# One-hot products of a source's three parts added in one PSUM bank, in a graph network kernel on one core

## The chip, the cores and the metric

The kernel runs on one core of a Trainium2 chip. The metric is the device time of one execution in microseconds (us); the times before and after are medians over runs. The engines are PE (the matrix engine, with its weight loads listed as PEld), DVE (vector), ACT (scalar), POOL and SP; SP and POOL also issue the transfers (DMAs). PE accumulates into PSUM, eight banks of 2 KB per partition, from which ACT and DVE copy results out.

## The reference

A graph of 6250 nodes (128 features) and 206250 edges, sorted by destination. Three attention layers (GATv2), then a small network, each with a residual and a layer norm:

```python
xl = (x @ Wl + bl).reshape(n, heads, outc)
e_feat = leaky_relu(xl[src] + (x @ Wr + br).reshape(n, heads, outc)[dst], 0.2)
logits = einsum('ehc,hc->eh', e_feat, att)
a = exp(logits - segment_max(logits, dst)[dst])
a = a / segment_sum(a, dst)[dst]
out = segment_sum(xl[src] * a[:, :, None], dst) + bias     # 4, 4 and 1 heads
...
e_aggr = segment_sum(edge_attr, dst) / maximum(count, 1)   # 96 edge features
h = concat([x, e_aggr, u[batch]]) @ W1 + b1                # 256 columns
h = relu(batch_norm(h)) @ W2 + b2
```

Everything is float32. The costly part is `xl[src]`: each destination needs the transformed rows of its 33 sources on average.

## The kernel before

**Blocks and slots.** The nodes are ranked by how many sources need a gather and cut into 49 blocks of 128 destinations, one per partition (`NB = 49`). A destination's sources lie in slots. Sources are divided by node number into 16 windows of 3 blocks of 128 nodes (the last of 4). Of each window a destination's first source goes into a window slot; all other sources go into its rest list, whose length `KR[b]` is 9 to 47 by block. So a block has 17 slots in the tile `ga` (its own row and 16 window slots) and `KR[b]` gathered slots in the tiles `g`.

**Window slots without a gather** (`windows`, L662). The table `tab` in SBUF holds all 49 source blocks, each value as a sum of three bf16 parts (`table`, L894: a cast on ACT L904, a subtraction on DVE L906, and so on, three parts in turn for up to `TS = 6` blocks at a time). A one-hot matrix `oh` of a block and window selects the row. PE multiplies one-hot by table block, 128 x (3 x 132) columns into a bank `pg` (L681), adding the window's three blocks there (129 in place of 132 columns in the last layer, with one head). ACT casts the bank to bf16 `raw` (L683); the three parts of three windows are then added by three products with a bf16 identity into the bank `ps` (L670), which ACT copies to `ga` (L671). The eight PSUM banks are: `pa` 2, `pt` 1, `pp` 2, `pg` 2, `ps` 1.

**Gathered slots** (`gather`, L631): one indirect transfer per slot, issued by POOL (L639), from the rows of all nodes in DRAM.

**The steps.** Each layer runs over the 49 blocks, in program order on each engine (an order written out by hand, nothing is moved). A step works on several blocks at once: `n2` (two ahead) starts its gathers and its windows 0 to 8, `c` gets its weights (exp on ACT, L714) and its weighing (`weigh`, L716: multiplications on DVE L722, sums over slots on PE L726), `c0` (one behind) is combined (moments with a square root on ACT L139, used by DVE at L144) and multiplied for the next layer (transpose L162, ACT L167, products L168 and L169, copy L171); then `n2`'s windows 9 to 15. The logits of `n1` (one ahead) stand on DVE in three pieces between these (L696 to L700). The order within a step:

```python
if c: c.weights()
if n2: n2.windows(tab, n2.oh, range(0, WH))
if n1: n1.logits(slice(1, 2))
if c: c.weigh()
if c0: c0.combine()
...
if c0: c0.output(); c0.products()
if n2: n2.windows(tab, n2.oh, range(WH, NW))
```

In the first layer each step also fetches a block's record (L776), unpacks it (L780) and builds its one-hots on DVE; later layers load the one-hots from DRAM. Every third step edge features are loaded (L846) and summed (L873). In the last layer the residual and the small network's hidden products (L1037 to L1054) hang on each step.

**The prologue** (up to 551 us) finds the sources of each node from the sorted edges and classifies them in seven groups of seven blocks (`classify`, L374): window slots by a masked maximum, the rest list by pairs of MAX (eight largest, L401) and MATCH_REPLACE (L403) up to `KL = 48` entries. It also computes layer 1's products (`first_sources`, L340), checks that the destinations are sorted (L432) and ranks the nodes. After it come the opening of the first layer (small memsets L812 to L817, records, loads, table) and then the steps; each later layer has its own opening with loads and a new table.

Of the kernel before, what the change touches and what calls it, by code (L numbers as in the profile page):

```python
# [20 lines left out]
P = 128  # L21
N, E, F, FE = 6250, 206250, 128, 96
NB = (N + P - 1) // P
NPAD = NB * P
# [9 lines left out]
WB = 3  # L34
NW = NB // WB
# [9 lines left out]
ROFF = tuple(sum(KR[:b]) for b in range(NB + 1))  # L45
KMAX = max(KD)
KEY = 128
KL = 48
RCLIP = KR[0] + 1
NBIN = RCLIP + 2  # L50
NT = (E + P - 1) // P
# [9 lines left out]
def chunks(b):  # L61

    n = min(EP, KM[b]) or EP
    r = KD[b] - n
    m = -(-r // EP)
    return [(0, n)] + [(n + r * i // m, r * (i + 1) // m - r * i // m) for i in range(m)]


TL = 13
TS = 6  # L70
WH = 9
TPW = P + max(LW)

# [14 lines left out]
def gnn_kernel(ctx: ExitStack, tc: tile.TileContext, t, out):  # L88
# [11 lines left out]

    ident = const.tile([P, P], F32, name="ident")
    make_identity(nc, ident)
    identb = const.tile([P, P], BF16, name="identb")
    nc.vector.tensor_copy(identb, ident)
# [14 lines left out]
    rec = dram.tile([NPAD, RW], F32, name="rec")  # L119

    ox = [None] + [dram.tile([NPAD, LW[l]], F32, name=f"ox{l}") for l in (1, 2)]
    ohd = dram.tile([NPAD, NB * P], BF16, name="ohd")
    pkd = dram.tile([NB * NW, P], BF16, name="pkd")
    hd = dram.tile([P, 2, NPAD], F32, name="hd")
# [53 lines left out]
    degs = const.tile([P, NB], F32, name="degs")  # L178
    first = const.tile([P, NB], F32, name="first")
    nfast = const.tile([P, 1], I32, name="nfast")  # L180
    bparts, wcat, attb, cbc, gcol, vs3 = ([] for _ in range(6))
    with tc.tile_pool(name="pre", bufs=1) as rp, tc.tile_pool(name="prew", bufs=2) as rw, \
            tc.tile_pool(name="n0", bufs=3) as np0, tc.tile_pool(name="n0p", bufs=2, space=PSUM) as npp, \
# [181 lines left out]
                nc.gpsimd.memset(wc[:, 1, w:w + 1], float(N - WBLK[w][0] * P - 256 + 1000))  # L365

        def rank_constants():
            for b in range(NB):
                nc.gpsimd.memset(kr[:, b:b + 1], float(KR[b]))
                nc.gpsimd.memset(kd[:, b:b + 1], float(KD[b]))  # L370
                nc.gpsimd.memset(km[:, b:b + 1], float(min(EP, KM[b])))
            nc.gpsimd.memset(onesq, 1.0)

        def classify(q):  # L374
# [19 lines left out]
            for j in range(UQ):  # L394
                v = key[:, j, :]
                s = 0
                for w in range(0, NW, 8):
                    nc.vector.match_replace(rest[:, j, s, :], top[:, j, w:w + 8], v, 0.0)
                    v, s = rest[:, j, s, :], 1 - s
                for k in range(0, KL, 8):  # L400
                    nc.vector.max(lst[:, j, k:k + 8], v)  # L401
                    if k + 8 < KL:
                        nc.vector.match_replace(rest[:, j, s, :], lst[:, j, k:k + 8], v, 0.0)  # L403
                        v, s = rest[:, j, s, :], 1 - s
            cls = rw.tile([P, UQ, CW_], F32, name="cls")
            any_ = rw.tile([P, UQ, NW], F32, name="any_")
            nc.vector.tensor_tensor(any_, top, wc[:, 0:1, :].to_broadcast([P, UQ, NW]), op=ALU.is_ge)
# [21 lines left out]
        bad = rp.tile([P, 5], F32, name="bad")  # L429
        falls = rp.tile([PP, W], BF16, name="falls")  # L430

        def sorted_check():  # L432
# [3 lines left out]
            nc.vector.memset(bad, 0.0)  # L436
            nc.vector.tensor_tensor(falls, d2[:, 1:], d2[:, :W], op=ALU.is_lt)
            nc.vector.tensor_reduce(bad[:PP, 0:1], falls, AX.X, ALU.max)

# [10 lines left out]
        for q in range(NQB):  # L450
            if q + 1 < NQB:
                find(q + 1, wins[q + 1])
            degrees(q)
            if q + 2 < NQB:
                wins.append(search(q + 2))
            if q == 0:
                finish += [weights(1), weights(2)]
            if q + 1 < NQB:
                for b in range((q + 1) * UQ, (q + 2) * UQ):
                    first_sources(b)  # L460
            classify(q)
            if q == 0:
                finish[1]()
                finish[2]()
            if q == 1:
                sorted_check()
                rank_constants()
# [140 lines left out]
    class Block:  # L608
# [52 lines left out]

        def windows(self, tab, oh, ws):  # L662


            k, X = self.k, self.X

            def add(w0, n, raw):
                ps = k.ps.tile([P, 3, X], F32, name="ps", padded_shape=[P, 3, XM])
                for i in range(3):
                    nc.tensor.matmul(ps[:, :n, :], lhsT=identb, rhs=raw[:, :n, i, :], start=i == 0, stop=i == 2)  # L670
                nc.scalar.copy(self.ga[:, 1 + w0:1 + w0 + n, :], ps[:, :n, :])  # L671

            todo = None
            for w0 in range(ws.start, ws.stop, 3):
                n = min(3, ws.stop - w0)
                raw = k.raw.tile([P, 3, 3, X], BF16, name="raw", padded_shape=[P, 3, 3, XM])
                for w in range(w0, w0 + n):
                    pg = k.pg.tile([P, 3, X], F32, name="pg", padded_shape=[P, 3, XM])
                    for j, s in enumerate(WBLK[w]):
                        o = j * NW + w if j < WB else WB * NW + j - WB  # L680
                        nc.tensor.matmul(pg, lhsT=oh[:, o, :], rhs=tab[:, s, :, :],  # L681
                                         start=j == 0, stop=s == WBLK[w][-1])
                    nc.scalar.copy(raw[:, w - w0, :, :], pg)  # L683
                    if todo:
                        add(*todo)
                        todo = None
                todo = w0, n, raw
            add(*todo)

        def logits(self, which):  # L690

# [68 lines left out]
    def slots_path():  # L760

        with ExitStack() as s:
            k = Pools(s, "sl", (("one", 1, 0), ("ga", 3, 0), ("big", 6, 0), ("wk", 2, 0), ("wk3", 3, 0),
                                ("ohp", 2, 0), ("pa", 2, 1), ("pt", 1, 1), ("pp", 2, 1), ("pg", 2, 1),
                                ("ps", 1, 1), ("raw", 2, 0)))
            one = k.one


# [4 lines left out]
            def record(c):  # L773

                c.rc = k.rcp.tile([P, RW], F32, name="rc")
                nc.gpsimd.indirect_dma_start(  # L776
                    out=c.rc, out_offset=None, in_=rec,
                    in_offset=bass.IndirectOffsetOnAxis(ap=ids_i[:, c.b:c.b + 1], axis=0))

            def unpack(c):  # L780
                b, o = c.b, LW[0] + F
                nc.sync.dma_start(out=rows(xp, b), in_=c.rc[:, LW[0]:o])
                nc.scalar.copy(sres[:, ROFF[b]:ROFF[b + 1]], c.rc[:, o:o + KR[b]])
# [23 lines left out]
                nc.sync.dma_start(out=c.oh.rearrange("p j d -> p (j d)"), in_=rows(ohd, c.b))  # L807


            NE = max(len(chunks(b)) for b in range(NB))  # L810
            off, cap = (one.tile([P, NE, NB], F32, name=v) for v in ("off", "cap"))
            nc.gpsimd.memset(off, 0.0)  # L812
            nc.gpsimd.memset(cap, float(E - EP))
            for b in range(NB):
                for i, (o, n) in enumerate(chunks(b)):
                    nc.gpsimd.memset(off[:, i, b:b + 1], float(o))
                    nc.gpsimd.memset(cap[:, i, b:b + 1], float(E - n))  # L817
# [75 lines left out]

            def table(l, c, loads):  # L894

                tab = one.tile([P, NB, 3, F + HEADS[l]], BF16, name="tab", padded_shape=[P, NB, 3, XM])
                done = 0
                for q, m, tf in loads:
                    for p in range(0, m, TS):
                        u = min(TS, m - p)  # L900
                        x = tf[:, p:p + u, :]
                        for i in range(3):
                            part = tab[:, q + p:q + p + u, i, :]
                            nc.scalar.copy(part, x)  # L904
                            if i < 2:
                                nc.vector.tensor_sub(x, x, part)  # L906
                        n = NW if q + p + u == NB else (q + p + u) // WB
                        n -= (n - done) % 3 if n < NW else 0
                        if n > done:
                            c.windows(tab, c.oh, range(done, n))  # L910
                            done = n
                return tab

            def layer(l, between, end):
# [589 lines left out]
```

## Time and profile before

| | |
|---|---|
| median of 17 runs | 7128.93 us (7098.39 to 7156.67) |
| the profiled execution | 7120.84 us |
| its span | 7119.0 us |
| mean granted clock of PE | 0.809 |
| busiest engine | DVE, 4560.9 us |
| products of the windows (L681) | 7203, 1698.0 us busy |
| casts of them (L683) | 2352, 1131.6 us busy |
| identity products (L670) and copies (L671) | 2646, 625.3 us, and 882, 398.3 us busy |
| gathers' issues (L639) | 2796, 2676.0 us busy |

The span runs from the first to the last instruction. Busy time is a sum over instructions; matmuls overlap, and their ends are modelled. In a list of waits, "sd L144 <- ACT sd L139" means that the engine stood idle before L144 until L139 on ACT was done; "issue" is idle time that no wait in the profile explains, and "remote" a release whose sender could not be found. In a timeline the bracket gives idle time ahead of an instruction and what ended it. The granted clock is given in parts of full speed.

### The profile page before, as it was taken

The numbers are of one execution on the slowest core, as the hardware profiler recorded it, in microseconds if no ns is written. First come the engines' busy times: TensorE is split into PE (matmuls) and PEld (weight loads), VectorE is DVE, ScalarE is ACT, GpSimd is POOL, SyncE is SP. The second block draws the span as 40 slices with busy tenths as digits, with TensorE's granted clock in tenths as the row PEclk, the third lists the DMA queues.
The fourth block names the chain that finished last, engine by engine and source line by source line (L and its number), as shares of the span: only waits on it lengthen the run. The fifth ranks groups of instructions, "written<-read, shape, count | busy, mean of one in ns | idle before, by whom it ended". The sixth has DMA issues, their size and how long they took to land. (4 is left out here: it accounts for less than half of the span.)

```text
span 7119.0 us, 52212 instructions
## 1 busy us (share of the span) xinstructions
PE 4119.3 (58%) x15200; PEld 2024.4 (28%) x15200; DVE 4560.9 (64%) x6804; ACT 2389.8 (34%) x5024; POOL 3132.3 (44%) x3642
## 2 busy tenths in 40 slices
PE   2214646545666655565655566665657665666665
PEld 1112223222223322222322233332323332333333
DVE  7875657656667756565755666665667676676665
ACT  3203324323333333333433234333333332333332
POOL 4314453454444443445454444544444444444442
PEclk9996878777788877787877788887788887888877
DMA  2203333334333323333334333333333334333332
GB/s 61 60 18 112 102 90 109 102 94 94 99 106 106 118 86 111 81 91 89 96 87 87 98 87 101 89 103 84 92 92 100 99 87 90 101 100 86 97 89 85
DMA packets 307927, 654.28 MB, mean 92 GB/s; under 512 B 93492, under 2 KB 215367, under 8 KB 283954
## 3 DMA queue, kind: packets, MB, share of 16 engines
q0 software_dynamic: 116720, 302.44, 18.0%
q1 hardware_dynamic: 186482, 341.98, 14.2%
q10 hardware_dynamic: 4432, 6.43, 0.3%
q8 instruction: 126, 2.06, 0.1%
q14 instruction: 167, 1.37, 0.1%
HBM read 519.06 MB, written 131.50 MB: 91 GB/s over the span
## 5 line engine op out<-in xcount | busy, mean ns | idle before, releaser
L639 POOL DMA_INDIRECT g<-xl,sres x2796 | 2676.0, 957 | 2350.7 <-issue 879.9
L681 PE MATMUL pg<-tab,oh 128*128 128x396 bf16 (+1 forms) x7203 | 1698.0, 376 | 1234.0 <-ACT raw L683 555.8
L683 ACT CAST raw<-pg 128x396 bf16<-128x396 f32 (+1 forms) x2352 | 1131.6, 489 | 1645.4 <-remote 883.4
L681 PEld LDWEIGHTS <-oh 128*128 128x128 bf16 x7203 | 770.9, 108 | 2016.9 <-issue 1653.8
L670 PE MATMUL ps<-raw,identb 128*128 128x396 bf16 (+1 forms) x2646 | 625.3, 351 | 692.5 <-issue 336.3
L722 DVE TENSOR_TENSOR ga<-ga,q 128x2176 f32<-128x2176 f32 x147 | 355.3, 2417 | 850.1 <-ACT q L714 495.6
L699 DVE TENSOR_REDUCE q<-z 128x68 f32<-128x2176 f32 (+19 forms) x444 | 777.6, 1751 | 15.3
L697 DVE SCALAR_TENSOR_TENSOR z<-z,q 128x2176 f32<-128x2176 f32 (+11 forms) x444 | 774.2, 1744 | 15.3
L671 ACT COPY ga<-ps 128x396 f32<-128x396 f32 (+1 forms) x882 | 398.3, 452 | 730.6 <-remote 285.5
L726 PE MATMUL acc<-ga,ident 128*128 128x512 f32 (+1 forms) x1470 | 615.0, 568 | 42.9 <-issue 29.0
L726 PE MATMUL acc<-g,ident 128*128 128x512 f32 (+3 forms) x1590 | 625.1, 541 | 0.0
L670 PEld LDWEIGHTS <-identb 128*128 128x128 bf16 x2646 | 274.1, 106 | 1021.3 <-issue 913.2
L846 POOL DMA_INDIRECT g<-in_ea_dram,est_i x102 | 96.7, 948 | 973.3 <-PE acc L726 696.5
L696 DVE TENSOR_TENSOR z<-g,q 128x1152 f32<-128x1152 f32 (+12 forms) x297 | 418.6, 1410 | 81.1 <-DMA g<-xl,sres 34.3
L144 DVE RECIPROCAL sd<-sd 128x1 f32<-128x1 f32 x196 | 31.0, 158 | 654.9 <-ACT sd L139 593.8
L726 PEld LDWEIGHTS acc<-ga,ident 128*128 128x128 f32 x1470 | 298.2, 205 | 373.8 <-issue 359.6
L722 DVE TENSOR_TENSOR g<-g,q 128x1280 f32<-128x1280 f32 (+8 forms) x243 | 400.7, 1682 | 0.0
L873 PE MATMUL acc<-g,ident 128*128 128x480 f32 (+4 forms) x818 | 378.0, 623 | 15.5 <-issue 13.5
L168 PE MATMUL tp<-wcat,hT 128*128 128x260 f32 (+1 forms) x294 | 141.0, 572 | 395.3 <-ACT hT L167 323.3
L726 PEld LDWEIGHTS acc<-g,ident 128*128 128x128 f32 x1590 | 286.6, 190 | 281.0 <-issue 273.5
L696 DVE TENSOR_TENSOR z<-ga,q 128x2176 f32<-128x2176 f32 x147 | 353.7, 2406 | 0.2
L167 ACT ACTIVATE hT<-tp,gcol 128x128 f32<-128x128 f32 x98 | 44.8, 457 | 820.4 <-PE tp L162 433.7
(259 smaller groups left out, 3587.6 us busy)
## 6 DMA issues: line engine op xcount, KB each, us to landing
oh<-ohd SPq DMA_DIRECT2D x98, 1568.0 KB
ohd<-oh SPq DMA_DIRECT2D x49, 1568.0 KB
g<-xl,sres POOLq DMA_INDIRECT x2796
pr<-pkd SPq DMA_DIRECT2D x49, 512.0 KB
rec<-lin SPq DMA_DIRECT2D x49, 130.0 KB
ox<-lin SPq DMA_DIRECT2D x49, 130.0 KB
ox<-lin SPq DMA_DIRECT2D x49, 128.5 KB
xrs<-ox SPq DMA_DIRECT2D x98, 64.0 KB
```

What stands on the lines that cost most here:

```text
L168: nc.tensor.matmul(pl, lhsT=hT, rhs=wcat[l], start=True, stop=False)
L639: nc.gpsimd.indirect_dma_start(out=g[:, i, :], out_offset=None, in_=xl[self.l], in_offset=bass.IndirectOffsetOnAxis(ap=sres[:, j:j + 1], a ...
L670: nc.tensor.matmul(ps[:, :n, :], lhsT=identb, rhs=raw[:, :n, i, :], start=i == 0, stop=i == 2)
L671: nc.scalar.copy(self.ga[:, 1 + w0:1 + w0 + n, :], ps[:, :n, :])
L681: nc.tensor.matmul(pg, lhsT=oh[:, o, :], rhs=tab[:, s, :, :], start=j == 0, stop=s == WBLK[w][-1])
L683: nc.scalar.copy(raw[:, w - w0, :, :], pg)
L696: nc.vector.tensor_add(z, g[:, :, :F], self.xrb.unsqueeze(1).to_broadcast([P, n, F]))
L697: nc.vector.scalar_tensor_tensor(z, z, 0.0, self.att.unsqueeze(1).to_broadcast([P, n, F]), op0=ALU.max, op1=ALU.mult)
L699: nc.vector.tensor_reduce(lg[:, cs, :], z.rearrange("p k (h c) -> p k h c", h=H), AX.X, ALU.add)
L722: nc.vector.tensor_mul(gh, gh, lg[:, c:c + n, :].unsqueeze(3).to_broadcast([P, n, H, F // H]))
L726: nc.tensor.matmul(self.acc[:, :r, :], lhsT=ident, rhs=g[:, i:i + r, :F], start=c + i == 0, stop=c + i + r == K1)
L873: nc.tensor.matmul(self.acc[:, :r, :], lhsT=ident, rhs=ea[:, i:i + r, :], start=o + i == 0, stop=o + i + r == K)
```

## The change

- **Windows.** The three parts are no longer three column ranges of one product. For each window PE makes one product of 128 x 132 for each source block and part, and all nine (twelve in the last window) add into the same slot of a bank. Three windows lie in one bank `pg`, and ACT copies the bank to `ga`. The bf16 identity, the tile `raw`, the bank `ps`, the casts and the identity products are gone; `pg` has three banks. A block has 147 products in place of 49 + 18.
- **Rest lists.** `KL` is 24 in place of 48: three pairs of MAX and MATCH_REPLACE per block. What is left over is stored to DRAM (`rst`). The six blocks with more than 24 rest sources fetch that row with a further gather (`record`) and extract the remaining entries when they are unpacked.
- **Prologue and opening.** The small memsets of the edge offsets move from the first layer's opening to `rank_constants`; the load for the check of the order moves ahead of the check; the first products of block 48 move behind the classification of the sixth group.
- **Table.** `TS` is 7, so there are 8 groups in place of 11, and the three parts of neighbouring groups are interleaved: each turn does part 1 of a group, part 2 of the one before and part 3 of the one before that. The first block's windows follow one turn later.

```diff
-KL = 48
+KL = 24
-TS = 6
+TS = 7
...
         def rank_constants():
+            nc.gpsimd.memset(eoff, 0.0)
+            nc.gpsimd.memset(ecap, float(E - EP))
             for b in range(NB):
...
+                for i, (o, n) in enumerate(chunks(b)):
+                    nc.gpsimd.memset(eoff[:, i, b:b + 1], float(o))
+                    nc.gpsimd.memset(ecap[:, i, b:b + 1], float(E - n))
...
                 for k in range(0, KL, 8):
                     nc.vector.max(lst[:, j, k:k + 8], v)
-                    if k + 8 < KL:
-                        nc.vector.match_replace(rest[:, j, s, :], lst[:, j, k:k + 8], v, 0.0)
-                        v, s = rest[:, j, s, :], 1 - s
+                    nc.vector.match_replace(rest[:, j, s, :], lst[:, j, k:k + 8], v, 0.0)
+                    v, s = rest[:, j, s, :], 1 - s
+            nc.sync.dma_start(out=rst[q * UQ * P:(q + 1) * UQ * P, :].rearrange("(b p) f -> p b f", p=P),
+                              in_=rest[:, :, 1 - s, :])
...
             if q == 0:
                 finish += [weights(1), weights(2)]
+                sorted_load()
             if q + 1 < NQB:
-                for b in range((q + 1) * UQ, (q + 2) * UQ):
+                for b in range((q + 1) * UQ, min((q + 2) * UQ, NB - 1)):
                     first_sources(b)
             classify(q)
+            if q + 2 == NQB:
+                first_sources(NB - 1)
...
         def windows(self, tab, oh, ws):
             k, X = self.k, self.X
-            def add(w0, n, raw):
-                ps = k.ps.tile([P, 3, X], F32, name="ps", padded_shape=[P, 3, XM])
-                for i in range(3):
-                    nc.tensor.matmul(ps[:, :n, :], lhsT=identb, rhs=raw[:, :n, i, :], start=i == 0, stop=i == 2)
-                nc.scalar.copy(self.ga[:, 1 + w0:1 + w0 + n, :], ps[:, :n, :])
-            todo = None
             for w0 in range(ws.start, ws.stop, 3):
                 n = min(3, ws.stop - w0)
-                raw = k.raw.tile([P, 3, 3, X], BF16, name="raw", padded_shape=[P, 3, 3, XM])
+                pg = k.pg.tile([P, 3, X], F32, name="pg", padded_shape=[P, 3, XM])
                 for w in range(w0, w0 + n):
-                    pg = k.pg.tile([P, 3, X], F32, name="pg", padded_shape=[P, 3, XM])
-                    for j, s in enumerate(WBLK[w]):
+                    todo = [(j, i) for j in range(len(WBLK[w])) for i in range(3)]
+                    for j, i in todo:
                         o = j * NW + w if j < WB else WB * NW + j - WB
-                        nc.tensor.matmul(pg, lhsT=oh[:, o, :], rhs=tab[:, s, :, :],
-                                         start=j == 0, stop=s == WBLK[w][-1])
-                    nc.scalar.copy(raw[:, w - w0, :, :], pg)
-                    if todo:
-                        add(*todo)
-                        todo = None
-                todo = w0, n, raw
-            add(*todo)
+                        nc.tensor.matmul(pg[:, w - w0, :], lhsT=oh[:, o, :], rhs=tab[:, WBLK[w][j], i, :],
+                                         start=(j, i) == todo[0], stop=(j, i) == todo[-1])
+                nc.scalar.copy(self.ga[:, 1 + w0:1 + w0 + n, :], pg[:, :n, :])
...
+                if KR[c.b] > KL:
+                    c.keys = k.rcp.tile([P, 2, KMAX], F32, name="keys", bufs=1)
+                    nc.gpsimd.indirect_dma_start(
+                        out=c.keys[:, 0, :], out_offset=None, in_=rst,
+                        in_offset=bass.IndirectOffsetOnAxis(ap=ids_i[:, c.b:c.b + 1], axis=0))
...
             def table(l, c, loads):
                 tab = one.tile([P, NB, 3, F + HEADS[l]], BF16, name="tab", padded_shape=[P, NB, 3, XM])
-                done = 0
-                for q, m, tf in loads:
-                    for p in range(0, m, TS):
-                        u = min(TS, m - p)
-                        x = tf[:, p:p + u, :]
-                        for i in range(3):
-                            part = tab[:, q + p:q + p + u, i, :]
-                            nc.scalar.copy(part, x)
-                            if i < 2:
-                                nc.vector.tensor_sub(x, x, part)
+                groups = [(q + p, tf[:, p:min(p + TS, m), :]) for q, m, tf in loads for p in range(0, m, TS)]
+                done = ready = 0
+                for i in range(len(groups) + 3):
+                    upto = ready
+                    for part in range(3):
+                        if 0 <= i - part < len(groups):
+                            o, x = groups[i - part]
+                            to = tab[:, o:o + x.shape[1], part, :]
+                            nc.scalar.copy(to, x)
+                            if part < 2:
+                                nc.vector.tensor_sub(x, x, to)
+                            else:
+                                ready = o + x.shape[1]
...
```

More of the change, by code (lines that the diff above doesn't have):

```diff
@@ L102, in gnn_kernel @@
     make_identity(nc, ident)
-    identb = const.tile([P, P], BF16, name="identb")
-    nc.vector.tensor_copy(identb, ident)
     ones = const.tile([1, P], F32, name="ones")
@@ L121, in gnn_kernel @@
     ox = [None] + [dram.tile([NPAD, LW[l]], F32, name=f"ox{l}") for l in (1, 2)]
+    rst = dram.tile([NPAD, KMAX], F32, name="rst")
     ohd = dram.tile([NPAD, NB * P], BF16, name="ohd")
@@ L180, in gnn_kernel @@
     nfast = const.tile([P, 1], I32, name="nfast")
+    NE = max(len(chunks(b)) for b in range(NB))
+    eoff, ecap = (const.tile([P, NE, NB], F32, name=v) for v in ("eoff", "ecap"))
     bparts, wcat, attb, cbc, gcol, vs3 = ([] for _ in range(6))
@@ L430, in gnn_kernel, with sorted_load @@
         falls = rp.tile([PP, W], BF16, name="falls")
-        def sorted_check():
+        def sorted_load():
             nc.sync.dma_start(out=d2[:, :W], in_=t["dst"].rearrange("(p w) -> p w", p=PP))
@@ L436, in sorted_check @@
             nc.vector.memset(bad, 0.0)
+        def sorted_check():
             nc.vector.tensor_tensor(falls, d2[:, 1:], d2[:, :W], op=ALU.is_lt)
@@ L763, in slots_path @@
             k = Pools(s, "sl", (("one", 1, 0), ("ga", 3, 0), ("big", 6, 0), ("wk", 2, 0), ("wk3", 3, 0),
-                                ("ohp", 2, 0), ("pa", 2, 1), ("pt", 1, 1), ("pp", 2, 1), ("pg", 2, 1),
-                                ("ps", 1, 1), ("raw", 2, 0)))
+                                ("ohp", 2, 0), ("pa", 2, 1), ("pt", 1, 1), ("pp", 2, 1), ("pg", 3, 1)))
             one = k.one
@@ L782, in unpack @@
                 nc.sync.dma_start(out=rows(xp, b), in_=c.rc[:, LW[0]:o])
-                nc.scalar.copy(sres[:, ROFF[b]:ROFF[b + 1]], c.rc[:, o:o + KR[b]])
+                n = min(KL, KR[b])
+                nc.scalar.copy(sres[:, ROFF[b]:ROFF[b] + n], c.rc[:, o:o + n])
+                if KR[b] > KL:
+                    m = KR[b] - KL
+                    mr = -(-m // 8) * 8
+                    lst = k.rcp.tile([P, 32], F32, name="lst", bufs=1)
+                    for i in range(0, mr, 8):
+                        a = i // 8 % 2
+                        nc.vector.max(lst[:, i:i + 8], c.keys[:, a, :])
+                        if i + 8 < mr:
+                            nc.vector.match_replace(c.keys[:, 1 - a, :], lst[:, i:i + 8], c.keys[:, a, :], 0.0)
+                    lst_i = k.rcp.tile([P, 32], I32, name="lst_i", bufs=1)
+                    nc.vector.tensor_copy(lst_i[:, :m], lst[:, :m])
+                    nc.vector.tensor_scalar(lst_i[:, :m], lst_i[:, :m], KEY.bit_length() - 1, None,
+                                            op0=ALU.arith_shift_right)
+                    nc.vector.tensor_scalar(lst[:, :m], lst_i[:, :m], -1.0, float(N), op0=ALU.mult, op1=ALU.add)
+                    nc.scalar.copy(sres[:, ROFF[b] + KL:ROFF[b + 1]], lst[:, :m])
                 c.pk = c.rc[:, o + KL:]
@@ L807, in one_hot_load @@
                 nc.sync.dma_start(out=c.oh.rearrange("p j d -> p (j d)"), in_=rows(ohd, c.b))
[L810 to L817, printed above, removed]
+            off, cap = eoff, ecap
             io_k = one.tile([P, EP], F32, name="io_k")
@@ L896, in table @@
                 tab = one.tile([P, NB, 3, F + HEADS[l]], BF16, name="tab", padded_shape=[P, NB, 3, XM])
-                done = 0
-                for q, m, tf in loads:
-                    for p in range(0, m, TS):
-                        u = min(TS, m - p)
-                        x = tf[:, p:p + u, :]
-                        for i in range(3):
-                            part = tab[:, q + p:q + p + u, i, :]
-                            nc.scalar.copy(part, x)
-                            if i < 2:
-                                nc.vector.tensor_sub(x, x, part)
[L907 to L911, printed above, removed]
+                groups = [(q + p, tf[:, p:min(p + TS, m), :]) for q, m, tf in loads for p in range(0, m, TS)]
[11 more added lines that the diff above has]
+                                ready = o + x.shape[1]
+                    n = NW if upto == NB else min(upto // WB, NW - 1)
+                    n -= (n - done) % 3 if n < NW else 0
+                    if n > done:
+                        c.windows(tab, c.oh, range(done, n))
+                        done = n
                 return tab
```

## The prediction

> **What bounds the kernel now.** I read the page's busy times first, then a table by stage (each row: stretch, length, then busy time of PE, PEld, DVE, ACT, POOL, granted clock, DMA share, GB/s), then the waits, then single stalls.
>
> ```profile
> PE 4119.3 (58%) x15200; PEld 2024.4 (28%) x15200; DVE 4560.9 (64%) x6804; ACT 2389.8 (34%) x5024; POOL 3132.3 (44%) x3642
> ```
> ```profile
> 0.00:535.00 535.00, 126.70 (x292) 59.60 (x292) 422.31 (x1489) 103.20 (x187) 158.80 (x340) 1.00 0.18 46
> 535.00:672.00 137.00, 51.87 (x194) 25.90 (x194) 57.94 (x98) 44.72 (x93) 68.22 (x266) 0.60 0.41 117
> 672.00:2777.00 2105.00, 1243.40 (x4644) 597.40 (x4642) 1352.66 (x1644) 716.46 (x1549) 968.80 (x1007) 0.79 0.35 102
> ...
> 2903.00:4900.00 1997.00, 1257.97 (x4605) 603.61 (x4604) 1249.35 (x1405) 694.85 (x1414) 913.63 (x962) 0.81 0.33 92
> ...
> 5050.00:7001.00 1951.00, 1271.30 (x4860) 645.82 (x4860) 1324.71 (x1821) 709.72 (x1554) 837.94 (x885) 0.83 0.34 93
> ```
>
> No engine is full. The three long rows are the 147 steps: 6053 us, 41.2 each. DVE has 1352.66 + 1249.35 + 1324.71 = 3926.7 us of work there (26.7 a step) and stands idle 2126 us; the other stages take 1066 us. So the question is what DVE waits for.
>
> ```profile
> DVE sd L144 <- ACT sd L139: 593.8, 68, 41.6
> DVE ga L722 <- ACT q L714: 495.6, 40, 43.4
> DVE ga L722 <- issue: 354.4, 36, 39.3
> ...
> ACT raw L683 <- remote: 883.4, 193, 22.0
> ACT raw L683 <- PE pg L681: 552.4, 823, 7.5
> ...
> POOL g L639 <- PE acc L726: 781.2, 48, 30.2
> ```
>
> (Total us, times, longest.) DVE waits for a square root (655 us in all before L144) and the exp (850 before L722). Both stand on ACT in program order, behind the casts of the products, which themselves wait 1436 us for PE. POOL's gathers wait for products that free their buffers: later in the same chain. ACT is only a third busy, but it hands on late. One such stall:
>
> ```profile
> 3029.32 0.49 ACT L683 CAST raw<-pg 128x396 bf16<-128x396 f32 x1 [0.94 <-PE pg L681]
> ...
> 3033.65 0.49 ACT L683 CAST raw<-pg 128x396 bf16<-128x396 f32 x1 [3.84 <-remote]
> ...
> 3036.38 0.49 ACT L671 COPY ga<-ps 128x396 f32<-128x396 f32 x1 [2.24 <-remote]
> 3036.92 0.49 PE L670 MATMUL ps<-raw,identb 128*128 128x132 bf16 x3 [6.39 <-ACT ga L671]
> ```
>
> PE had finished both products by its records (the last identity products ended at 3030.5), yet ACT was released 3 and 6 us later, while gathers ran. What delays the signal the trace doesn't say; such stalls come where PE has stopped for want of ACT.
>
> **The windows, all 147 steps.** Before, a block has 49 products of 396 columns, 18 identity products, 16 casts and 6 copies: 22 times PE hands to ACT. After, 147 products of 132 columns (129 in layer 3) go straight into three slots of a bank, with 6 copies of 396. ACT sheds 2352 casts, 1131.6 us in all, 7.7 a step. PE sheds 49 x 0.165 + 15 x 0.165 + 3 x 0.06 = 10.8 us at full clock (spacing of products in bursts) and gets 147 x 0.06 = 8.8. The 0.06 is from three 132-column products, each with its own weights, that took 0.34 us at full clock, the last of them 0.22; at half clock (the row at 3036.92: 0.49 for three) it is about 0.11, 16.5 us a step against 21. This is the nearest row; the far end, weights and product strictly in turn, is the last rival.
>
> In layer 2 of 3 the timeline has, as a mean over steps, 13.6 us from the exp to the last copy of the first half, and 8.7 us from the first to the last copy of the second. PE needs 81 x 0.06 = 4.9 and 66 x 0.06 = 4.0 us, plus one copy of 0.49: 8 and 4 us sooner. PE runs 81 products with nothing to wait for (three banks of 27, freed by copies of 0.49 us every 1.6 us), so only the last copy of a half is a hand-over at which PE stops. The added wait, a group's first product for the copy three groups back, has transposes and the weighed sums behind it on PE; it costs something only where ACT is held over 3 us, as a cast held it before.
>
> So the wait for the square root, 4.5 us a step, nearly goes (655 to about 125), and that for the exp, 5.8 a step, falls to about 300 in all, since a step's remaining hand-overs (last copies, transposes for the next layer) can still be late. The other 621 us of DVE's idle time (2126 - 655 - 850; the last layer's hidden products L1043 and statistics L1054, edge loads) I take at 545. That leaves about 970: steps 3927 + 970 = 4897, 33.3 us each. Bounds: idle 450 if all of PE's lateness goes; no gain if late signals simply move.
>
> **Rule against row.** The three products above show 60 ns each at full clock. The Trainium skill, "TensorE: Matmul & The Clock Gate", section "Back-to-back issue gap", gives about 81 ns for a sustained stream of weight load and 128-column product; and "Perfetto Trace Analysis", section "Matmuls", says larger matmuls are more efficient where possible, which speaks against cutting 396 columns into 132. By 81 ns a block's windows take 11.9 us, longer than before; if half of the extra 3.1 a step showed, the estimate would be 230 us higher, about 6010. I keep the row, as a burst of three is all this trace has.
>
> **Prologue (0 to 551).** DVE is 422 of 535 us busy and the path.
>
> ```profile
> L401 DVE MAX8 lst<-rest 128x8 f32<-128x66 f32 x294 | 67.6, 230 | 13.3 <-DVE rest L403 3.3
> ...
> L403 DVE MATCH_REPLACE8 rest<-lst,rest 128x66 f32<-128x66 f32 x245 | 52.0, 212 | 0.0
> L403 DVE MATCH_VALUE_LOAD rest<-lst,rest 128x8 f32 x245 | 22.6, 92 | 9.8 <-DVE lst L401 1.4
> ```
>
> Lists of 24 need 147 of each: 147 x 0.230 + 98 x 0.304 = 63.6 us less, about 70 with the gaps between, and 3 for shorter list arithmetic. Block 48's first products come after the sixth classification: the 23.4 us that DVE stood at L173 for the copy of L171 go. The destination load moved ahead takes 10.3 us of waiting at L437. Sum 107. The seven stores of the rests (0.3 to 0.5 us of SP each, as its other stores here) have the next use of that buffer two classifications off; at worst 2 us each. The later products of block 48 lie on PE, ACT and SP beside the last classification (50 us of DVE); if not hidden, 5.
>
> **Openings.** 102 + 102 small memsets (6.7 us) and two large ones leave POOL's path before the first record gathers: 8 us less; in the prologue POOL is 159 of 535 us busy, and the window gathers queued behind them wait at most 7. The table stage takes about 60 us in each layer: 33 casts of 0.68 (22 us) and 22 subtractions of 0.77 (17 us) in turn, with the loads. With 8 groups interleaved, ACT's 22 plus fill, and the loads (20 us), give about 30: 30 less in the first opening, 35 in each later one. Bounds: 0, if PE's signals come late here as in the steps, and 40, if only the loads remain. So prologue and first opening 672 - 107 - 38 = 527, the two others 126 to 91 and 150 to 115, tail 118: 851 in place of 1066.
>
> **Long lists.** Six blocks (24 to 47 keys) get one more gather (0.95 us of POOL each) and 8 MAX and 2 replacements with four small operations on DVE, about 10 us in layer 1's steps; bounds 5 and 25, should the gather land late. I take 15.
>
> **Sum.** 851 + 4897 + 15 = 5763 of span, 1.84 outside it, and 8 because the median (7128.93) lies above the profiled 7120.84: 5773, so about 5780.
>
> **Rivals.**
> - *Gathers bound the steps.* 19 a step at 0.95 and a 0.30 gap, with stores and loads 26.3 us, and each first gather waits for products that free a buffer: 781 + 697 us, 10.05 a step. If that wait stays, 36.4 x 147 = 5350, in all 6220. For it: the waits' length. Against: those products are themselves late behind exp.
> - *Late signals move* to the last copies and transposes. Exp's wait stays, the square root's halves: steps 6053 - 330, in all 6600. For it: the transposes' own waits (ACT hT L167 <- PE tp L162, 433.7 us).
> - *DVE fills up*, idle 450: 5250. Against: L1043 and L1054 alone waited 472 us, for PE and for ACT.
> - *The casts were hidden anyway*: steps stay, only the 215 us of openings and prologue come: about 6930.
> - *Slower: PE becomes the bound.* Weighed sums, edge sums and layer products keep PE busy 12 us a step; with p a product, 12 + 147p passes the step that breaks even, (6053 + 215) / 147 = 42.6, at p = 0.208. Weight load (0.108) and product (0.217) in turn give 0.325: 59.8 a step, about 9650. Any starved PE counts here. Against: 0.06 in the burst.
>
> **How the numbers follow.** Chances: forecast 0.42, gathers 0.16, late signals 0.17, DVE full 0.11, hidden casts 0.07, slower 0.07. 5250 to 6650 leaves out the last two and a little of the fast case. Under 0.2% can't be told from no change here: 0.92 faster, 0.01 same, 0.07 slower.
>
> **What would show it.** ACT about 1.1 ms less busy; product spacing near 0.06; waits before L144's reciprocal under 200 us and before L722's first multiply near 300; prologue ending near 444. It is wrong if the products stand wider than 0.2 us, or if ACT's copies show the old waits for PE.

## The result

The changed kernel takes 7370.69 us (median of 8 runs, 7346.48 to 7392.19) against 7124.61 (the kernel before, now the median of 46 runs): a ratio of 1.0344, with an interval of 1.0326 to 1.0362. It is slower by 3.4%; I had said 5780. The profiled execution took 7378.23 us, its span 7376.4.

First the busy times, then three groups of instructions on the profile page of the changed kernel (busy time and mean ns of one; after the bar the idle time ahead of them and what ended most of it):

```profile
PE 4048.2 (55%) x26960; PEld 2557.5 (35%) x26960; DVE 4491.6 (61%) x6472; ACT 1250.0 (17%) x2651; POOL 3128.2 (42%) x3648
...
L685 PE MATMUL pg<-tab,oh 128*128 128x132 bf16 (+1 forms) x21609 | 1799.1, 238 | 1715.6 <-issue 1643.4
L685 PEld LDWEIGHTS <-oh 128*128 128x128 bf16 x21609 | 1494.0, 105 | 1985.7 <-issue 1927.7
L687 ACT COPY ga<-pg 128x396 f32<-128x396 f32 (+1 forms) x882 | 388.5, 452 | 4038.5 <-remote 2711.3
```

All the work that was to go has gone: ACT is 1140 us less busy (2389.8 to 1250.0). But ACT now stands idle for 4038.5 us ahead of 882 copies, and PE, in the middle of its products, stands idle for 1715.6 us, 1643.4 of them with no wait that the profile can name. The waits that I expected to fall (total us, times, longest):

```profile
ACT ga L687 <- remote: 2711.3, 205, 65.3
...
ACT ga L687 <- PE pg L685: 1105.4, 464, 44.4
POOL g L652 <- PE acc L725: 1103.8, 69, 30.4
DVE sd L143 <- ACT sd L138: 1035.3, 53, 42.3
...
DVE ga L721 <- ACT q L713: 641.5, 59, 54.2
```

ACT's waits for PE's window products rose to 3817 us from 1961 (1436 ahead of the casts and 525 ahead of the copies), POOL's for PE's sums from 781 to 1104, DVE's for the square root from 655 to 1035. Only DVE's idle time ahead of L721 fell a little, from 850 to 820 (641.5 of it for the exp).

Where the time went by stage follows from the timeline: the first exp comes at 552.7 us in place of 671.9; the three rows of steps, from a layer's first exp to its last, take 2142, 2051 and 2253 us in place of 2105, 1997 and 1950. So 119 us were won ahead of the steps and 394 lost in them, 303 of these in the last layer.

The timeline of the changed kernel shows how. First a view from 2984 on, in which products still come in a row and then stop doing so:

```profile
2983.82 1.74 PE L685 MATMUL pg<-tab,oh 128*128 128x132 bf16 x25
...
2985.95 0.22 PE L685 MATMUL pg<-tab,oh 128*128 128x132 bf16 x1 [0.39 <-issue]
...
2988.12 0.49 ACT L687 COPY ga<-pg 128x396 f32<-128x396 f32 x1 [9.31 <-remote]
```

Then the same stretch from 3000 on. POOL's gathers are in flight until about 3016:

```profile
3004.76 0.94 POOL L652 DMA_INDIRECT g<-xl,sres  x1 [0.30 <-issue]
3005.63 0.27 PE L685 MATMUL pg<-tab,oh 128*128 128x132 bf16 x1 [1.80 <-issue]
...
3007.03 0.10 PEld L685 LDWEIGHTS <-oh 128*128 128x128 bf16 x1 [2.69 <-issue]
...
3007.73 0.27 PE L685 MATMUL pg<-tab,oh 128*128 128x132 bf16 x1 [1.83 <-issue]
...
3009.13 0.10 PEld L685 LDWEIGHTS <-oh 128*128 128x128 bf16 x1 [2.00 <-issue]
...
3010.54 0.27 PE L685 MATMUL pg<-tab,oh 128*128 128x132 bf16 x1 [2.54 <-issue]
3010.55 0.10 PEld L685 LDWEIGHTS <-oh 128*128 128x128 bf16 x1 [1.31 <-issue]
...
3011.23 0.27 PE L685 MATMUL pg<-tab,oh 128*128 128x132 bf16 x1 [0.42 <-issue]
...
3012.27 0.94 POOL L652 DMA_INDIRECT g<-xl,sres  x1 [0.30 <-issue]
...
3016.14 1.01 PE L725 MATMUL acc<-ga,ident 128*128 128x512 f32 x1 [0.19 <-issue]
...
3017.55 0.88 ACT L687 COPY ga<-pg 128x396 f32<-128x396 f32 x2 [28.94 <-remote]
...
3026.34 8.60 PEld L685 LDWEIGHTS <-oh 128*128 128x128 bf16 x147
3026.35 8.77 PE L685 MATMUL pg<-tab,oh 128*128 128x132 bf16 x147
```

From about 2986 on PE takes its weight loads and products one at a time, sometimes a few together, and about 0.7 us or a small multiple of it apart. No record is missing: the 21609 products are 147 in each of the 147 steps. ACT gets two copies released together after 28.94 us of idle time, just after the gathers have ended. Ten microseconds later, with no gather in flight, PE does 147 products in 8.77 us, 0.060 each: the spacing that I had taken from a burst of three.

The granted clock and the bytes don't explain this. In the table by stage (PE, PEld, DVE, ACT, POOL, granted clock, DMA share, GB/s), a slow stretch and the fast one:

```profile
3000.00:3008.00 8.00, 1.47 (x6) 0.63 (x6) 0.00 (x0) 0.00 (x0) 6.17 (x7) 0.50 0.26 59
...
3027.00:3034.00 7.00, 7.00 (x123) 7.00 (x121) 6.72 (x11) 3.67 (x7) 0.00 (x0) 1.00 0.88 240
```

At half clock the prediction's own row gives about 0.11 us a product, not a tick of 0.7 for each instruction, and the fast stretch has four times the bytes moving beside it.

A number from all steps, worked out from the timeline: the time between the copies of two neighbouring groups where ACT waited for the second, that is, 27 products and 27 weight loads. Without gathers the median is 1.58 us (193 cases). With gathers in flight in over 30% of that time the mean is 13.2 us, the median 10.4 (194 cases). This mean is somewhat high, since of two copies released together only the first counts, with the time of both.

### The profile page after: what moved, and what is told of

The parts are those of the page before. It is cut to its first block, busy times and chain, and to the rows that moved or that the text cites. A ratio compares the mean times of both kernels' runs of the same rounds, so it can differ in the third digit from the quotient of the medians.

```text
span 7376.4 us, 72554 instructions
## 1 busy us (share of the span) xinstructions
PE 4048.2 (55%) x26960; PEld 2557.5 (35%) x26960; DVE 4491.6 (61%) x6472; ACT 1250.0 (17%) x2651; POOL 3128.2 (42%) x3648
## 3 DMA queue, kind: packets, MB, share of 16 engines
q1 hardware_dynamic: 192866, 343.03, 13.9%
## 4 chain that ended last, share of the span: by engine, by line
PE 29%; DVE 27%; issue 21%; another core or an unknown queue 16%; ACT 4%; DMA 2%; POOL 1%; DVEq 0%; SPq 0%; ACTq 0%; POOLq 0%
PE pg L685 11%; PE acc L725 9%; PE acc L885 5%; DVE z L696 4%; DVE q L698 4%; DVE z L695 4%; DVE ga L721 3%; DVE g L721 2%; PE tp L1066 1%; ACT ga L687 1%; DVE mk L395 1%; POOL g L652 1%; DVE top L398 1%; PE tp L167 1%
## 5 line engine op out<-in xcount | busy, mean ns | idle before, releaser
L685 PE MATMUL pg<-tab,oh 128*128 128x132 bf16 (+1 forms) x21609 | 1799.1, 238 | 1715.6 <-issue 1643.4
L685 PEld LDWEIGHTS <-oh 128*128 128x128 bf16 x21609 | 1494.0, 105 | 1985.7 <-issue 1927.7
L687 ACT COPY ga<-pg 128x396 f32<-128x396 f32 (+1 forms) x882 | 388.5, 452 | 4038.5 <-remote 2711.3
L725 PE MATMUL acc<-ga,ident 128*128 128x512 f32 (+1 forms) x1470 | 802.1, 690 | 354.1 <-DVE ga L721 200.0
L721 DVE TENSOR_TENSOR ga<-ga,q 128x2176 f32<-128x2176 f32 x147 | 355.2, 2416 | 820.4 <-ACT q L713 641.5
L698 DVE TENSOR_REDUCE q<-z 128x68 f32<-128x2176 f32 (+19 forms) x444 | 777.6, 1751 | 15.3
L725 PE MATMUL acc<-g,ident 128*128 128x512 f32 (+3 forms) x1590 | 645.9, 554 | 16.8 <-issue 16.8
L725 PEld LDWEIGHTS acc<-ga,ident 128*128 128x128 f32 x1470 | 343.2, 242 | 824.2 <-issue 621.3
L885 PE MATMUL acc<-g,ident 128*128 128x480 f32 (+4 forms) x818 | 435.5, 682 | 101.8 <-issue 98.8
L725 PEld LDWEIGHTS acc<-g,ident 128*128 128x128 f32 x1590 | 295.7, 196 | 312.5 <-issue 300.3
L721 DVE TENSOR_TENSOR g<-g,q 128x1280 f32<-128x1280 f32 (+8 forms) x243 | 400.7, 1682 | 0.0
L885 PEld LDWEIGHTS acc<-g,ident 128*128 128x128 f32 x818 | 197.2, 249 | 346.5 <-issue 337.5
L1066 PE MATMUL tp<-xT,w1x 128*128 128x128 f32 x196 | 72.4, 469 | 419.9 <-ACT eT L1059 390.3
L1066 PEld LDWEIGHTS tp<-xT,w1x 128*128 128x128 f32 x196 | 45.4, 288 | 452.7 <-ACT eT L1059 409.2
```

What stands on the lines that cost most here:

```text
L685: nc.tensor.matmul(pg[:, w - w0, :], lhsT=oh[:, o, :], rhs=tab[:, WBLK[w][j], i, :], start=(j, i) == todo[0], stop=(j, i) == todo[-1])
L687: nc.scalar.copy(self.ga[:, 1 + w0:1 + w0 + n, :], pg[:, :n, :])
L698: nc.vector.tensor_reduce(lg[:, cs, :], z.rearrange("p k (h c) -> p k h c", h=H), AX.X, ALU.add)
L721: nc.vector.tensor_mul(gh, gh, lg[:, c:c + n, :].unsqueeze(3).to_broadcast([P, n, H, F // H]))
L725: nc.tensor.matmul(self.acc[:, :r, :], lhsT=ident, rhs=g[:, i:i + r, :F], start=c + i == 0, stop=c + i + r == K1)
L885: nc.tensor.matmul(self.acc[:, :r, :], lhsT=ident, rhs=ea[:, i:i + r, :], start=o + i == 0, stop=o + i + r == K)
```

## The experiments

Two theories stood at the start. A: while POOL's gathers are in flight, PE pays for each instruction, however narrow, and the change makes 294 of 134. B: the loss lies elsewhere in the change. Times of one group of runs are compared on the same chip; the groups fell on four chips, which I call P, Q, R and S. Which chip gave the result above isn't on record; the kernel before takes 7125 us there.

### On chip P: windows apart from the rest, and gathers taken away

`oldwin` is the changed kernel with the windows of before; `newwin` is the reverse:

```diff
 # oldwin: after.py with
-                nc.tensor.matmul(pg[:, w - w0, :], lhsT=oh[:, o, :], rhs=tab[:, WBLK[w][j], i, :], ...)
+                nc.tensor.matmul(pg, lhsT=oh[:, o, :], rhs=tab[:, s, :, :], ...)
+                nc.scalar.copy(raw[:, w - w0, :, :], pg)
+                nc.tensor.matmul(ps[:, :n, :], lhsT=identb, rhs=raw[:, :n, i, :], ...)
...
```

The `bulk` pair takes POOL's row gathers away, after and before:

```diff
-                for i in range(n):
-                    j = ROFF[b] + c - SW + i
-                    nc.gpsimd.indirect_dma_start(
-                        out=g[:, i, :], out_offset=None, in_=xl[self.l],
-                        in_offset=bass.IndirectOffsetOnAxis(ap=sres[:, j:j + 1], axis=0))
+                nc.sync.dma_start(out=g, in_=xl[self.l][(b % (NB - n)) * P:(b % (NB - n) + n) * P, :].rearrange("(k p) f -> p k f", p=P))
```

> The changed kernel with the windows of before (396-column products, 16 casts, 18 identity products a block); lists, prologue and table as changed. Theory A: while POOL's gathers are in flight, PE pays per instruction, whatever its width, and the 294 weight loads and products a block in place of 134 are the loss. Then this kernel keeps the gain up to the first exp (119 us earlier in the trace) and about 18 us at the second opening: about 6980 us, and ACT waits no more than before for PE. Rival B: the loss comes from elsewhere in the change (longer lists unpacked in the steps, the new table, the extra gathers): about 7300 or more.

> The kernel of before with the windows of the change alone (147 products of 132 columns a block, three slots a bank, no casts). Theory A: the whole loss is here, so about 7124 + 390 = 7510 us, with 27 products of a group taking over 10 us where gathers are in flight and 1.6 us where not. Rival B: the windows by themselves gain, as I forecast: under 7000.

> The changed kernel with each tile of gathered slots filled by one load from SP of as many consecutive rows (same bytes, no list of rows, so the slots hold other rows than the lists say): POOL issues no row gathers. Theory A: PE runs its products at 0.06 us throughout, the steps come near DVE's work, about 33 us each: 5800 us. Rival C: PE is slow because of the bytes that are written into SBUF beside it, whoever issues them: slow stretches stay and the time is above 6900. Rival D: PE is slow by the length of its own program (more instructions to fetch): above 7000.

> The kernel of before with the same loads from SP in place of POOL's row gathers. Theory A: its late signals go too, steps of 33 to 36 us, so 6000 to 6300 us, and more than the changed kernel with the same loads. Rivals C and D: above 6900, no change worth the name.

Measured: the kernel before took 5294.03 us here, not 7125. `oldwin` took 5107.23 (ratio 0.9648, 0.9632 to 0.9664), `newwin` 5269.59 (0.9954, 0.9938 to 0.9971), `bulk_after` 4995.68 (0.9437), `bulk_before` 5205.66 (0.9833). Every expectation in microseconds missed, because on this chip PE isn't slow under gathers at all. The groups of `newwin` on chip P:

```profile
L670 PE MATMUL pg<-tab,oh 128*128 128x132 bf16 (+1 forms) x21609 | 1453.9, 231 | 178.1 <-ACT tab L887 104.0
...
L672 ACT COPY ga<-pg 128x396 f32<-128x396 f32 (+1 forms) x882 | 393.6, 452 | 864.0 <-PE pg L670 853.6
```

The same 21609 products, with the same gathers beside them, have 178 us of idle time ahead of them in place of 1716, and the profile names what ended all of it. 27 products take a median of 1.58 us under gathers as well. So the price under gathers isn't a property of the program alone.

Chip P tells a second thing. Here DVE is 86 to 89% busy, and the steps of `bulk_before` and `bulk_after` are alike: 29.07, 26.81 and 32.09 us a step in the three layers against 29.05, 26.72 and 32.68. Where PE isn't slowed, the 16 casts and 18 identity products of a block are hidden, and the new windows are worth 0.5% of the kernel. What the change gains on this chip is the prologue, the table and the opening (`oldwin`, 187 us). The changed kernel itself wasn't run on chip P.

### On chip Q: the changed kernel again, without gathers, and with the old windows

> The changed kernel unchanged, beside the kernel before on the same chip. In the first four runs the kernel before took 5294 us, where it had taken 7125, and PE ran 27 products in 1.6 us under gathers too. Theory A2: the price per PE instruction under gathers belongs to the chip or its state, not to the program. Where the kernel before takes about 5290, this takes about 5290 x 0.9954 x 0.9648 = 5085; where it takes about 7125, this takes about 7370. Rival B2: the windows cost by themselves everywhere; above 5290 also there.

> The changed kernel with each tile of gathered slots filled by one load from SP of as many consecutive rows, so the slots hold other rows than the lists say. Theory A2: about 4996 where the kernel before takes 5290; between 5000 and 5800 where it takes 7125, since no gather of POOL is left to slow PE. Rival C: the slow state has nothing to do with POOL's gathers: above 6700 where the kernel before takes 7125.

> The changed kernel with the windows of before. Theory A2: 5107 where the kernel before takes 5290; about 6980, and so 5% under the changed kernel, where it takes 7125. Rival B: above 7300 there.

Measured, with the kernel before at 7186.91: the changed kernel 7445.50 (1.036, 1.0331 to 1.039), `oldwin` 7051.51 (0.9809, 0.9774 to 0.9845), `bulk_after` 5022.25 (0.6986, 0.6961 to 0.7012).

So the split is clear on this chip. The windows cost 394 us (7445.5 - 7051.5), the rest of the change gains 135 (7186.9 - 7051.5), and rival B falls. And with the gathers replaced by loads from SP the same program takes 5022 us, within 0.6% of its time on chip P (4996). On chip Q the row gathers cost the changed kernel 2423 us (7445.5 - 5022.25); on chip P they cost the kernel before only 88 (5294.03 - 5205.66). Between the chips the kernel before differs by 1893 us and `oldwin` by 1944. So nearly the whole difference lies in what POOL's gathers do to PE. Rivals C (bytes written beside PE) and D (length of PE's program) fall with it: the bytes and PE's program were the same.

### On chip R: width, number, and kind of transfer

```diff
 # narrow
+                        x = X if (j, i) in (todo[0], todo[-1]) else 32
-                        nc.tensor.matmul(pg[:, w - w0, :], ..., rhs=tab[:, WBLK[w][j], i, :],
+                        nc.tensor.matmul(pg[:, w - w0, :x], ..., rhs=tab[:, WBLK[w][j], i, :x],
 # twoparts
-                    todo = [(j, i) for j in range(len(WBLK[w])) for i in range(3)]
+                    todo = [(j, i) for j in range(len(WBLK[w])) for i in range(2)]
 # pooldirect
-                    j = ROFF[b] + c - SW + i
-                    nc.gpsimd.indirect_dma_start(out=g[:, i, :], ...)
+                    r = (b + c + i) % NB * P
+                    nc.gpsimd.dma_start(out=g[:, i, :], in_=xl[self.l][r:r + P, :])
 # f32win
-                tab = one.tile([P, NB, 3, F + HEADS[l]], BF16, name="tab", ...)
+                tab = one.tile([P, NB, X], F32, name="tab", ...)      # loaded by SP, no parts
-                oh = k.ohp.tile([P, NB, P], BF16, name="oh")
+                oh = k.ohp.tile([P, NB, P], F32, name="oh")
+                        nc.tensor.matmul(pg[:, w - w0, :], lhsT=oh[:, o, :], rhs=tab[:, b, :], ...)
```

(`f32win` also has one buffer fewer for `pr` and for a tile of the tail, for room.)

> The changed kernel with all products of a window but its first and last cut to 32 of 132 columns (the missing columns leave the sums of the window slots incomplete): the same number of weight loads and products, 115 of 147 of them a quarter as wide. Where POOL's gathers slow PE (the kernel before at about 7150): theory A, price per instruction: 7300 to 7450. Rival: price per column read or written: the slow stretches shrink with the columns, under 7000. Where the kernel before takes about 5290: 5000 to 5090 by either.

> The changed kernel with only the first two of the three bf16 parts of a source multiplied (window slots lose their last bits): 98 products and 98 weight loads a block in place of 147 and 147. Theory A: from 7445 at 294 instructions a block and 7051 at 134 on the slow chip, 2.46 us for each instruction of a block: 7445 - 98 x 2.46 = 7200. Rival: PE's instructions are not what the steps wait for: 7400. Where the kernel before takes 5290: 5020 to 5085.

> The changed kernel with each row gather of POOL replaced by one plain transfer from POOL of 128 consecutive rows for that slot (as many transfers and bytes from the same engine's queue, no list; the slots hold other rows). If it is transfers that POOL issues, list or no list, that slow PE: 7200 to 7450 on the chip where the kernel before takes 7150. If it is the lists: 5000 to 5400 there, as with the loads from SP (5022). Where the kernel before takes 5290: about 5050.

> The changed kernel with the table and one-hots in float32: 49 weight loads and 49 products of 132 columns a block (98 instructions, fewer than the 134 of before), no parts, no casts, the table loaded straight into place; the one-hots take twice the bytes. Theory A: on the slow chip 7051 - 36 x 2.46 = 6960, less some 50 us of table work, 6900; where the kernel before takes 5290: about 5000. Rival: a float32 product costs PE so much more, or the one-hots' loads collide so much with the gathers, that it is no faster than with the windows of before: 7050 and more, or 5107 and more.

Measured, with the kernel before at 7196.94:

| run | time, us | ratio (interval) |
|---|---|---|
| narrow | 7494.98 | 1.0413 (1.0369 to 1.0458) |
| twoparts | 6835.03 | 0.9497 (0.9455 to 0.9538) |
| pooldirect | 5061.12 | 0.7032 (0.7001 to 0.7063) |
| f32win | 6965.73 | 0.9689 (0.9631 to 0.9746) |

`narrow` settles the kind of price: with 115 of 147 products cut to a quarter, nothing is gained. PE's busy time on products falls from 1799.1 to 1184.0 us, its idle time in them rises from 1715.6 to 2302.7 (on chip Q the changed kernel has 1808.9 and 1965.0). The groups of `narrow`:

```profile
L686 PE MATMUL pg<-tab,oh 128*128 128x32 bf16 (+2 forms) x21609 | 1184.0, 197 | 2302.7 <-issue 2190.3
L686 PEld LDWEIGHTS <-oh 128*128 128x128 bf16 x21609 | 946.1, 102 | 2511.1 <-issue 2442.7
```

`twoparts` shows that the number counts, and that my linear price was wrong: 98 instructions fewer gave 610 us against the changed kernel on chip Q, not 241. The slope of 2.46 came from comparing with the old windows, which have fewer instructions but 22 hand-overs to ACT instead of 6; that these extra hand-overs make the slope too small is likely, but no run separates it. At equal hand-overs an instruction of a block costs 6.2 us of the kernel (610 / 98).

| run (chips Q, R) | instructions between two copies | mean us, gathers in flight | us each | median us without gathers |
|---|---|---|---|---|
| changed kernel | 54 | 13.9 | 0.26 | 1.58 |
| narrow | 54 | 15.3 | 0.28 | 0.97 |
| twoparts | 36 | 10.0 | 0.28 | 1.32 |
| f32win | 36 | 8.7 | 0.24 | 2.02 |

(Time between neighbouring copies as above.) Without gathers the time follows the work; with them the mean follows the number of instructions, 0.24 to 0.28 us each whatever their width or type. If the copies for which ACT didn't wait are counted too, the second ones of two released together among them, the means are 13.1, 12.4, 8.5 and 8.6 us, and the price is 0.23 or 0.24 us in all four. Single cases scatter widely around these means.

`pooldirect` is the surprise: as many transfers from the same queue, with the same bytes, and nothing is slow. Its product group:

```profile
L683 PE MATMUL pg<-tab,oh 128*128 128x132 bf16 (+1 forms) x21609 | 1423.5, 229 | 127.3 <-ACT tab L917 67.7
```

So it isn't POOL's queue, nor the bytes, but transfers by list or the scattered rows that they read.

`f32win` is the one that beats both kernels here with the whole sum kept: 6965.73. I had counted 98 instructions a block; the profile lists 14406 products and as many loads, 98 of each, so a float32 product is issued as two. So it has 196 instructions, as many as `twoparts`, and takes 131 us more. The count alone doesn't give a kernel's time: a group without gathers takes 2.02 us here and 1.32 there, and the one-hots have twice the bytes. No run separates these.

### On chip S: lists of consecutive rows

```diff
+            k.seq = one.tile([P, NB], I32, name="seq")
+            nc.gpsimd.iota(k.seq, pattern=[[P, NB]], base=0, channel_multiplier=1)
...
-                    j = ROFF[b] + c - SW + i
+                    j = (b + c + i) % NB
...
-                        in_offset=bass.IndirectOffsetOnAxis(ap=sres[:, j:j + 1], axis=0))
+                        in_offset=bass.IndirectOffsetOnAxis(ap=self.k.seq[:, j:j + 1], axis=0))
```

> The changed kernel with the row gathers of POOL kept as transfers by list, but with lists of 128 consecutive node numbers, the same rows as in the run with plain transfers from POOL (the slots hold other rows than the kernel needs). If the list itself is what slows PE (the engine's way of issuing it), 7300 to 7450 on the chip where the kernel before takes about 7190, against 5061 with plain transfers. If scattered rows in memory do it: near 5061. Where the kernel before takes 5290: about 5085 by either.

Measured: 7459.18 us, with the kernel before at 7208.30 (1.035, 1.032 to 1.038). Same rows and bytes as `pooldirect`, only by list, and the loss is all there:

```profile
L685 PE MATMUL pg<-tab,oh 128*128 128x132 bf16 (+1 forms) x21609 | 1821.3, 237 | 2064.8 <-issue 1986.1
```

It is the transfer by list, not where the rows lie, though `pooldirect` ran on chip R and this on S; both are chips where the kernel before takes about 7200. What POOL's queue moved is alike in number and bytes (packets, MB, share of 16 engines), first `pooldirect`, then `seqlist`:

```profile
q0 software_dynamic: 116912, 302.04, 20.5%
...
q0 software_dynamic: 116912, 302.04, 13.8%
```

What differs besides the list is how POOL issues: 0.55 us for a plain transfer in `pooldirect`, 0.95 for one by list. No run takes the two apart. But it isn't POOL's issuing alone: in the timeline above its last gather is issued at 3012.27 and done at 3013.21, while packets move until 3016 and PE's ticks of 0.7 us last until 3017.5. Nor is PE slow from the first packet on: packets of these gathers move from 2982 on, and PE still does 25 products in 1.74 us at 2983.82.

## Why the prediction was wrong

**Openings and prologue: nearly right at the first opening, too high at the later ones.** The first record's gather starts at 450.86 in place of 555.85, 105 us earlier; prologue and memsets were to give 115. The first table stage takes 47.1 us from first to last cast, not 30: ACT waits 17.3 us there for the loads, more than my sum left room for. The two others take 21 (59.3 and 60.0 before), better than my 30. But the second opening, from the last exp of a layer to the first of the next, fell by 18.6 us and the third by 0.5, not 35 each. Where PE isn't slow they fall by more than that: between `bulk_before` and `bulk_after` on chip P by 44.8 and 40.8. In all the change without its windows gained 135 us on chip Q, against 215 forecast.

**Product spacing: right in the burst, wrong where it counts.** 0.06 us held to the digit without gathers. The row came from a moment without them; under them it is 13.2 / 27 = 0.49 on average (0.46 with all copies counted), far beyond the 0.208 at which I had the kernel break even. My remark that "any starved PE counts here" named the case, but I gave it 7 in 100, because I looked for a price in weight loads or clock and not in gathers. The page's 81 ns for such a stream (the Trainium skill, "TensorE: Matmul & The Clock Gate", section "Back-to-back issue gap") was not met either: 60 ns over 147 products without gathers, about eight times as much on average with them.

**The step that failed** is the reading of the late signals: "such stalls come where PE has stopped for want of ACT". From it came that fewer hand-overs mean fewer stalls, and that 81 products in a row run free, at 0.06 us each. The runs show something else in its place: while transfers by list are in flight PE pays for each instruction, 13.2 us on average for 27 products and loads that take 1.58 without. With 6 hand-overs in place of 22 but 294 instructions in place of 134, the stalls grew. The trace of before had it. In the stall that I quoted, between the releases at 3029.32, 3033.65 and 3036.38 lie four loads and four products, then three and three: 4.33 / 8 and 2.73 / 6, 0.54 and 0.45 us an instruction. I saw 3 and 6 us of lateness and did not divide them by what PE had to do. Both signs that I had named for being wrong came: products wider apart than 0.2 us, and ACT's copies waiting for PE.

The late signals themselves are real and belong to the list transfers. In the changed kernel ACT waited ahead of 691 of its copies, and 320 of these began over 1 us after the modelled end of their last product; in `newwin` on chip P, none of 722 did; in `pooldirect`, 18 of 695. Whether such a signal is a product that was really done late, or one that was done and told late, stays open. In the stretch above the bank filled at 2985.95, counted by 27 products, was copied only at 3017.55, though by PE's own records all 27 products of the next bank came in between, and that bank was copied 0.4 us after it. By these records, part of the lateness there lies in the signal.

**DVE's idle time** was read rightly as waiting for the square root and the exp behind ACT's copies, and wrongly as ACT's doing: in `oldwin` on chip P, with all the casts on ACT and all the gathers by list, the two waits are 2.2 and 9.8 us in place of 655 and 850. On chip P, and on Q, R with the list transfers taken away, the steps are 27 to 33 us, with DVE nearly full. The 33.3 us a step of my forecast were there to be had, but by freeing PE, not ACT.

**Rivals.** That the casts were hidden is right where PE isn't slowed (0.5% on chip P). That late signals move to the remaining hand-overs is right for the exp, whose wait stayed (850 to 820 us); the square root's didn't halve but rose, from 655 to 1035. "PE becomes the bound" had the right direction and the wrong price: not weight load and product in turn at 0.325 everywhere, but 0.06 without list transfers and about 0.49 with them. That the gathers bound the steps isn't so where PE runs fast: POOL's wait for PE's sums falls from 781 us to 432 in `newwin` on chip P, with the same gathers. The unpacking of long lists can't cost much: `oldwin` has it and still gains 135 us on chip Q.

## What to carry to other kernels

Where signals come late after modelled ends, divide the time between two of them by the instructions that the engine had in between, over many cases: if the mean is the same for kernels with other widths and other counts, the number of instructions is what counts, and not their size. Where POOL gathers rows by list beside PE's work, on a chip that behaves like Q, R and S, count PE's instructions: fewer and wider products beat more and narrower ones even if they leave more for another engine to add up (on chip P it made 0.5%). And a price taken from a burst holds for the moments like that burst: look what else was in flight.

## What the runs showed of the hardware

- On chips Q and R, PE took 0.24 to 0.28 us on average for each weight load and product while POOL's transfers by list were in flight in over 30% of the time (ticks of 0.7 us in the stretch shown), whatever the width or type, against 0.03 without (1.58 / 54). On chip S lists of consecutive rows were as slow (7459 us). Plain transfers from POOL (5061 us) or loads from SP (5022) with the same bytes have no such price.
- On chip P the same programs have no such price: the kernel before takes 5294 us there, and 7187 to 7208 on the others. What sets the chips apart, and by what path a list reaches PE, stays open; no run here tells it.
- A float32 product of this kernel shows as two weight loads and two products in the trace (98 of each for 49 written).
- DVE's operations aren't slowed: its busy time is 4491.6 us in the changed kernel and 4477.2 with plain transfers.
